# Two transformer layers on one core: a written-out TensorE order and a minimum of negated scores in the first attention

## Chip, core and metric

The kernel runs on one core of a Trainium2 chip. Its time is the device time in microseconds (us) of one execution; several executions are measured and the median is given. The core has five engines with a program order of their own: TensorE (PE, matrix products; PEld is its weight load), VectorE (DVE), ScalarE (ACT), GpSimd (POOL) and SyncE (SP), which here issues the DMAs.

## What is computed

`x` has 4 batch rows of 256 tokens and 256 features. Everything is float32. Two pre-norm layers follow one another, each an attention and a feed-forward network:

```python
x = x + _L0_attn_ref(_layernorm(x), ...)   # 16 query heads, 8 key heads, RMS norm, RoPE, window 128
x = x + _L0_ffn_ref(_layernorm(x), ...)    # silu gate, 2 of 4 kept
x = x + _L1_attn_ref(_layernorm(x), ...)   # 16 heads, causal
x = x + _L1_ffn_ref(_layernorm(x), ...)    # silu gate, Walsh-Hadamard transform
```

The first attention, on which the change works mostly:

```python
q = jnp.einsum('btd,ndh->btnh', x, q_kernel)
k, v = jnp.einsum('bsd,ckdh->cbskh', x, kv_kernel)
q, k = rms_norm(q, q_norm_scale), rms_norm(k, k_norm_scale)
q, k = apply_rope(q, positions), apply_rope(k, positions)
mask = (j <= i) & (i - j < 128)
logits = jnp.einsum('btkgh,bskh->bkgts', qg * ATTN_SCALE, k)
probs = jax.nn.softmax(jnp.where(mask, logits, finfo.min), axis=-1)
enc = jnp.einsum('bkgts,bskh->btkgh', probs, v)
return jnp.einsum('btnh,nhd->btd', enc, out_kernel)
```

## The kernel before

**Steps of the first attention.** The work is cut into 16 units, numbered n = 4 b + g: batch row b and group g of 4 query heads with their 2 key heads. `pipelined` runs a loop over steps. In each step every stage handles the unit that lies its lag behind the step:

- `project` (lag 0): for each of the two 128-token blocks, two products, 512 columns of queries (`wq`) and 512 columns of keys and values (`wkv`), each as two matmuls into a PSUM tile `pj` of the pool's tag "half" (four buffers, shared with `tr_q`). DVE then writes `pj` times the sine and the cosine table (`qs`, `qc`, L466), ACT squares it (`sq`, L471) and copies the values (`v`).
- `rotate` (lag 0): DVE adds `qc` and the swapped `qs` (L484) and sums the squares (`ss`, L485). POOL makes `r`, the power -1/2 of the twelve mean squares of a token (L498, L501, L504), and multiplies the keys by it (L507). The queries' factors stay in `r`. From n = 6 on POOL also splits the queries into 16-bit planes (`qpl`), which a DMA transposes (`qplT`).
- `turn` (lag 1): the queries are transposed by TensorE (`tr_q`, n < 6) or put together from the DMA's planes by DVE (`qT`); the keys by TensorE (`tr_k`, L533), copied to `kT` by ACT (L534).
- `score` (lag 2): for each half of two heads, `probabilities`. TensorE makes the scores `sc` (L218, L219), a custom DVE instruction adds the mask, writes the sums to `p` and keeps the row's maximum `mx` (L221); DVE makes the bias `nb` = -`mx` times `r` (L228), or times the constant scale in the second attention (L226); ACT takes exp with the scale `r` and the bias `nb` and sums the rows (L231); DVE takes the reciprocal `rs` (L236), POOL multiplies `p` by it (L239).
- `split` (lag 3) and `join` (lag 4): POOL splits `p` into planes (`pl`, L245), a DMA transposes them (`plT`), ACT copies them to `pT` (L265).
- `attend` (lag 4): TensorE multiplies with `v` (`av`, L409, L413), ACT copies to `zT`. `out` follows in `behind`: `po`, one token block of one half of a batch row (L300), and DVE adds it to `x`.

**The order of the work.** `order` says in which order a step's stages are written, `(0, 5, 4, 3, 1, 2, 6)` here: project, join, split, score, rotate, turn, attend. A scheduler of the framework then puts the instructions of each engine in an order of its own; `tc.issue_after` holds an instruction behind another, and `manual_schedule`, for the steps of `in_order`, keeps an engine to the written order. The first attention has no such steps before, the second has (for TensorE). Each engine executes its instructions in the order in which they were built.

**The norm.** `moments(b)` gives mean and reciprocal deviation of a batch row, `normed(b)` subtracts and scales on DVE (`xn`, L172), transposes on TensorE (`tr_n`, L183) and copies on ACT (`xnT`). The row b + 1 is normed in `project` of the row b, with g = 1 (moments) and g = 2:

```python
                if g == 2 and b + 1 < B:
                    with tc.issue_after(last_of["qc"].ins):
                        xnT[b + 1] = normed(b + 1, factors[b + 1])
```

The second attention uses `probabilities` too, with `rq` None. The functions that the diff touches, and what calls them:

Of the kernel before, what the change touches and what calls it, by code (L numbers as in the profile page):

```python
# [21 lines left out]
F32 = mybir.dt.float32  # L22
BF16 = mybir.dt.bfloat16
U16 = mybir.dt.uint16
AF = mybir.ActivationFunctionType
ALU = mybir.AluOpType
AX = mybir.AxisListType

P = 128
B, T, D = 4, 256, 256  # L30
NT = T // P
NC = D // P
HD = 128
# [3 lines left out]
WINDOW = 128  # L37
LN_EPS = 1e-5
RMS_EPS = 1e-6
SCALE0 = 0.08838834764831845  # L40
SCALE1 = 0.08838834764831845
NEG0 = -1e30
NEG1 = -1e10


C_ID, C_HAD, C_M0, C_M1, C_END = 0, 128, 256, 640, 1024
# [3 lines left out]
def two_layers(ctx, tc, consts, tables, x, wq, wkv, wo, w_gate, w_up, w_down,  # L50
               w_k, w_q, w_v, w_o, w1, w3, w2, out):
    nc = tc.nc
# [92 lines left out]
    last_of = {}  # L145
# [60 lines left out]
    def probabilities(qT, kT, heads, mask, rq=None):  # L206


        p = work.tile([P, 2, 3 * P], F32, tag="p", name="p", bufs=4)
        mx = small.tile([P, 2, 2], F32, tag="mx", name="mx")  # L210
        nb = small.tile([P, 2, 2], F32, tag="nb", name="nb")
        sm = small.tile([P, 2, 2], F32, tag="sm", name="sm")
        rs = small.tile([P, 2, 2], F32, tag="rs", name="rs")
        rows = ((0, slice(0, P)), (1, slice(P, 3 * P)))
        for j in range(2):
            q, k = qT[:, heads[j], :], kT[:, heads[j] if rq is None else heads[0] // 2, :]
            sc = bank([3 * P], "sc")
            nc.tensor.matmul(sc[:, 0:P], lhsT=q[:, 0:P], rhs=k[:, 0:P], start=True, stop=True)  # L218
            nc.tensor.matmul(sc[:, P : 3 * P], lhsT=q[:, P:T], rhs=k, start=True, stop=True)  # L219
            for i, cols in rows:  # L220
                last_of["mx"] = nc.vector.tensor_tensor_reduce(  # L221
                    out=p[:, j, cols], in0=sc[:, cols], in1=mask[:, cols], scale=1.0,
                    scalar=-3.0e38, op0=ALU.add, op1=ALU.max, accum_out=mx[:, j, i : i + 1],
                )
        if rq is None:
            nc.vector.tensor_scalar_mul(nb, mx, -SCALE1)  # L226
        else:
            nc.vector.scalar_tensor_tensor(nb, mx, -1.0, rq, ALU.mult, ALU.mult)  # L228
        for j in range(2):
            for i, cols in rows:  # L230
                last_of["exp"] = nc.scalar.activation(  # L231
                    p[:, j, cols], p[:, j, cols], AF.Exp, bias=nb[:, j, i : i + 1],
                    scale=SCALE1 if rq is None else rq[:, j, i : i + 1],
                    accum_out=sm[:, j, i : i + 1],
                )
        nc.vector.reciprocal(rs, sm)  # L236
        for j in range(2):
            for i, cols in rows:
                nc.gpsimd.tensor_scalar(  # L239
                    p[:, j, cols], p[:, j, cols], rs[:, j, i : i + 1], 1.0, ALU.mult, ALU.mult  # L240
                )
        return p
# [86 lines left out]
    def attention0():  # L329
        with tc.tile_pool(name="attn0", bufs=2, reuse_waits="tile", side="right") as own:  # L330
# [10 lines left out]
                            tab[:, t], src.unsqueeze(1).to_broadcast([P, 2, HD]), scl, ALU.mult  # L341
                        )

            def project(n, _):
                b, g = divmod(n, 4)
                held = project0(own, xnT[b], g, cos_s, sin_s, n == 0)
                if g == 1 and b + 1 < B:
                    factors[b + 1] = moments(b + 1)
                if g == 2 and b + 1 < B:
                    with tc.issue_after(last_of["qc"].ins):  # L350
                        xnT[b + 1] = normed(b + 1, factors[b + 1])
                return held if n < 14 else rotated(n, held)

            def rotated(n, held):
# [7 lines left out]
            def turn(n, held):  # L362
                rot, qT_planes, v, r = held
                return *turn0(own, rot, qT_planes, half if 6 <= n < 14 else bank), v, r

            def score(n, held):
                qT, kT, v, r = held
# [52 lines left out]
            def out(b, t, gs, kept=False):  # L420
# [12 lines left out]
                for b in range(B) for k in range(2) for t in range(NT)  # L433
            }
            behind = {step: fns for step, fns in behind.items() if step < 16}
            behind[17] = [lambda _: xn_f.append(normed(0))]
            behind[19] = [lambda _: xn_f.append(normed(1)), *(out(3, t, (2, 3)) for t in range(NT))]
            pipelined(
                (project, rotate, turn, score, split, join, attend), (0, 0, 1, 2, 3, 4, 4),
                behind, (0, 5, 4, 3, 1, 2, 6),  # L440
            )

    def project0(own, xnT, g, cos_s, sin_s, first):
# [9 lines left out]
        parts = [(t, *part) for t in range(NT) for part in (queries, rest)]  # L453
        if first:
            parts = [(t, *part) for part in (queries, rest) for t in range(NT)]
        for t, w, hs in parts:
            qc, qs, sq = rot[t]
            pj = half([4, HD], "pj")
            n = hs.stop - hs.start
            for c in range(NC):  # L460
                last_of[0] = nc.tensor.matmul(  # L461
                    pj, lhsT=xnT[:, c, t * P : (t + 1) * P], rhs=w[:, g, c, :],
                    start=(c == 0), stop=(c == NC - 1),
                )
            for rot_to, tab in ((qs, sin_s), (qc, cos_s)):
                last_of["qc"] = nc.vector.tensor_tensor(  # L466
                    rot_to[:, hs], pj[:, 0:n],
                    tab[:, t, hs.start // 4, :].unsqueeze(1).to_broadcast([P, n, HD]),
                    ALU.mult,
                )  # L470
            nc.scalar.activation(sq[:, hs], pj[:, 0:n], AF.Square)  # L471
            if n == 2:
                last_of["v", t] = nc.scalar.copy(v[:, t, :, :], pj[:, 2:4])
        return rot, v

    def rotate0(rot, by_dma, first):

# [10 lines left out]
        if by_dma:  # L488

            planes = page_of_planes([P, NT, 2, 4 * HD], "qpl")  # L490
            for t, qc in enumerate(rot):
# [3 lines left out]
            nc.sync.dma_start_transpose(qT_planes, planes.rearrange("p t w n -> p (t w n)"))  # L495

        ve = small.tile([P, NT, 6], F32, tag="ve", name="ve")
        nc.gpsimd.tensor_scalar(  # L498
            ve[:, :, 0:4], ss[:, :, 0:4], 1.0, HD * RMS_EPS, ALU.mult, ALU.add
        )  # L500
        nc.gpsimd.tensor_scalar(  # L501
            ve[:, :, 4:6], ss[:, :, 4:6], 1.0 / HD, RMS_EPS, ALU.mult, ALU.add
        )
        nc.gpsimd.tensor_tensor(r.rearrange("p t h -> p (t h)"), ve.rearrange("p t h -> p (t h)"),  # L504
                                mhalf, ALU.pow)
        for t, qc in enumerate(rot):
            last_of["k"] = nc.gpsimd.tensor_tensor(  # L507
                qc[:, 4:6, :], qc[:, 4:6, :],
                r[:, t, 4:6].unsqueeze(2).to_broadcast([P, 2, HD]), ALU.mult,
            )  # L510
        return rot, qT_planes, r

    def turn0(own, rot, qT_planes, bank_of_k):
# [3 lines left out]
        for t, qc in enumerate(rot):  # L517
# [13 lines left out]
            tk = bank_of_k([2, P], "tr_k")  # L531
            for j in range(2):
                nc.tensor.transpose(tk[:, j, :], qc[:, 4 + j, :], ident)  # L533
            nc.scalar.copy(kT[:, :, cols], tk)  # L534
        return qT, kT


# [554 lines left out]
def _constants():  # L1092
# [7 lines left out]
    while len(h) < P:  # L1100
        h = np.block([[h, h], [h, -h]])
    c[:, C_HAD:C_M0] = h / np.float32(32)
    for at, window, neg in ((C_M0, WINDOW, NEG0), (C_M1, T, NEG1)):
        for n, (qb, kb) in enumerate(((0, 0), (1, 0), (1, 1))):
            i = qb * P + np.arange(P)[:, None]
            j = kb * P + np.arange(P)[None, :]
            ok = (j <= i) & (i - j < window)
            c[:, at + n * P : at + (n + 1) * P] = np.where(ok, 0.0, neg)
    frac = np.arange(0, HD, 2, dtype=np.float32) / np.float32(HD)
    angle = np.arange(T, dtype=np.float32)[:, None] / np.power(np.float32(10000.0), frac)  # L1110
    angle = angle.astype(np.float32)
# [60 lines left out]
```

## Time and profile before

| | |
|---|---|
| median of 3 runs | 731.75 us (731.65 to 732.66) |
| the profiled execution | 733.21 us, of which the span is 731.4 us |
| granted TensorE clock | 1.00 |
| busy: PE, PEld | 718.4, 572.4 us |
| busy: DVE, ACT, POOL | 476.0, 414.0, 367.3 us |
| the first attention | from the start to about 262 us |

The span goes from the first to the last instruction. A group's row gives the line, the engine, the operation, what it writes and reads, the shape, the number of instructions, their busy time in us and the mean of one in ns, and behind the second bar how long the engine was idle before them and what ended that. Matmuls are pipelined and their ends are modelled, so a duration on PE includes time in which its successor already runs.

### The profile page before, as it was taken

The page shows a single profiled execution, that of the slowest core. Times are in us where ns is not written, and L with a number is a line of the kernel's source. Part 1 is how long each engine was busy: PE and PEld are TensorE (multiplying, and loading weights), DVE is VectorE, ACT ScalarE, POOL GpSimd, SP SyncE. Part 2 cuts the span into 40 slices and gives each one's busy share as a digit, 9 for nine tenths or more (in the row PEclk, how much of TensorE's full clock was granted, in tenths as well). Part 3 has the DMA queues.
Part 4 walks back from the last instruction along what each step waited for, and adds up shares of the span by engine and source line. Part 5 has one row for each costly group of instructions (what it writes and reads, how often), then busy time and mean ns, then how long its engine had stood idle before and what let it go on. Part 6 is the DMA issues. An engine that isn't in the chain of part 4 may idle for free. (4 is left out here: it accounts for less than half of the span.)

```text
span 731.4 us, 10484 instructions
## 1 busy us (share of the span) xinstructions
PE 718.4 (98%) x3336; PEld 572.4 (78%) x3336; DVE 476.0 (65%) x1425; ACT 414.0 (57%) x984; POOL 367.3 (50%) x521
## 2 busy tenths in 40 slices
PE   9999999999999999999999999999999999999998
PEld 5556566656666778888887899999998889888886
DVE  6999877788887536987844556665553554635443
ACT  2487887767767962222357655555555557654331
POOL 1678878897799741011105566473636663802000
PEclk9999999999999999999999999999999999999999
DMA  8732345425355447000003334252425422401000
GB/s 324 301 65 45 64 83 92 88 53 99 73 93 102 73 75 227 16 14 15 9 7 58 66 65 130 58 117 44 125 48 116 117 44 45 89 13 30 0 30 29
DMA packets 138342, 57.42 MB, mean 79 GB/s; under 512 B 131504, under 2 KB 133680, under 8 KB 137520
## 3 DMA queue, kind: packets, MB, share of 16 engines
q1 hardware_dynamic: 138288, 56.77, 34.6%
q8 instruction: 26, 0.43, 0.2%
q14 instruction: 28, 0.23, 0.1%
HBM read 22.94 MB, written 1.05 MB: 33 GB/s over the span
## 5 line engine op out<-in xcount | busy, mean ns | idle before, releaser
L239 POOL TENSOR_SCALAR p<-p,rs 128x128 f32<-128x128 f32 (+1 forms) x256 | 114.2, 465 | 137.1 <-DVE rs L236 137.1
L265 ACT COPY pT<-plT 128x1536 uint16<-128x1536 uint16 (+1 forms) x62 | 93.6, 1566 | 10.0 <-DMA plT<-pl 10.0
L245 POOL TENSOR_SCALAR pl<-p 128x1536 uint16<-128x1536 uint16 x64 | 94.4, 1476 | 4.6 <-POOL p L239 0.5
L221 DVE CUSTOM_DVE_ANT_0 p<-sc,cst 128x128 f32<-128x128 f32 (+1 forms) x256 | 78.7, 352 | 12.4 <-PE sc L219 10.0
L231 ACT ACTIVATE p<-p,nb,r 128x128 f32<-128x128 f32 (+1 forms) x128 | 68.2, 535 | 20.2 <-DVE nb L228 20.2
L461 PE MATMUL pj<-wq,xnT 128*128 128x512 f32 x128 | 61.0, 595 | 1.4 <-DVE qT L523 1.1
L231 ACT ACTIVATE p<-p,nb 128x128 f32<-128x128 f32 (+1 forms) x128 | 56.4, 442 | 9.7 <-DVE nb L226 9.7
L461 PE MATMUL pj<-wkv,xnT 128*128 128x512 f32 x128 | 60.1, 592 | 0.0
L300 PE MATMUL po<-wo,zT 128*128 128x256 f32 x256 | 57.9, 379 | 0.0
L471 ACT ACTIVATE sq<-pj 128x512 f32<-128x512 f32 (+1 forms) x64 | 30.9, 490 | 42.8 <-DVE qc L466 42.4
L157 POOL TENSOR_SCALAR ve<-mv 128x2 f32<-128x2 f32 (+1 forms) x17 | 4.3, 253 | 99.6 <-DVE mv L153 99.0
L725 ACT COPY qk<-qk_x 128x512 f32<-128x512 f32 x16 | 9.4, 586 | 78.6 <-PE qk_x L945 42.0
L300 PEld LDWEIGHTS po<-wo,zT 128*128 128x128 f32 x256 | 48.3, 190 | 7.0 <-ACT kT L534 0.6
L461 PEld LDWEIGHTS pj<-wkv,xnT 128*128 128x128 f32 x128 | 24.3, 190 | 30.2 <-issue 28.5
L466 DVE TENSOR_TENSOR qs<-pj,sin_s 128x512 f32<-128x512 f32 (+1 forms) x64 | 35.3, 551 | 13.5 <-PE pj L461 12.9
L461 PEld LDWEIGHTS pj<-wq,xnT 128*128 128x128 f32 x128 | 23.5, 190 | 24.5 <-issue 20.1
L273 PE MATMUL av<-pT,v 128*128 128x256 f32 x128 | 38.4, 381 | 0.2 <-ACT zT L817 0.2
L245 POOL TENSOR_SCALAR qpl<-qc 128x1024 uint16<-128x1024 uint16 x20 | 28.8, 1453 | 18.9 <-PE av L413 8.2
L219 PE MATMUL sc<-kT,qT 128*128 128x256 f32 x128 | 38.3, 381 | 0.0
L219 PE MATMUL sc<-qk 128*128 128x256 f32 x128 | 38.2, 380 | 0.0
L854 DVE TENSOR_TENSOR x<-po,x 128x128 f32<-128x128 f32 x56 | 16.0, 285 | 33.1 <-PE po L849 33.1
L504 POOL TENSOR_TENSOR r<-ve,mhalf 128x12 f32<-128x12 f32 x16 | 36.6, 2290 | 0.8
(187 smaller groups left out, 1797.6 us busy)
## 6 DMA issues: line engine op xcount, KB each, us to landing
w<-in_w_dram SPq DMA_DIRECT2D x3, 1024.0 KB, 5.5
wq<-in_wq_dram SPq DMA_DIRECT2D x4, 512.0 KB, 7.6
wkv<-in_wkv_dram SPq DMA_DIRECT2D x4, 512.0 KB, 8.2
wo<-in_wo_dram SPq DMA_DIRECT2D x4, 512.0 KB, 10.2
w_qk<-in_w_q_dram SPq DMA_DIRECT2D x4, 512.0 KB, 4.3
w_qk<-in_w_k_dram SPq DMA_DIRECT2D x4, 512.0 KB, 5.2
w_v<-in_w_v_dram SPq DMA_DIRECT2D x4, 512.0 KB, 6.4
w_o<-in_w_o_dram SPq DMA_DIRECT2D x4, 512.0 KB, 6.3
```

The costliest lines, as they stand in the source:

```text
L219: nc.tensor.matmul(sc[:, P : 3 * P], lhsT=q[:, P:T], rhs=k, start=True, stop=True)
L221: last_of["mx"] = nc.vector.tensor_tensor_reduce(out=p[:, j, cols], in0=sc[:, cols], in1=mask[:, cols], scale=1.0, scalar=-3.0e38, op0=ALU ...
L231: last_of["exp"] = nc.scalar.activation(p[:, j, cols], p[:, j, cols], AF.Exp, bias=nb[:, j, i : i + 1], scale=SCALE1 if rq is None else rq ...
L239: nc.gpsimd.tensor_scalar(p[:, j, cols], p[:, j, cols], rs[:, j, i : i + 1], 1.0, ALU.mult, ALU.mult)
L245: last_of["planes"] = nc.gpsimd.tensor_scalar(o, i, 1.0, 1.0, ALU.mult, ALU.mult)
L265: copy(words.rearrange("p (n w) -> p w n", w=2), halves[:, :, js].rearrange("p w j n -> p w (j n)"),)
L273: nc.tensor.matmul(av, lhsT=v0, rhs=pT[:, 0:T], start=True, stop=False, skip_group_check=True)
L300: nc.tensor.matmul(po, lhsT=zTs[hd // 4][:, hd % 4, t * P : (t + 1) * P], rhs=w[:, hd, :], start=(hd == 0), stop=(hd == n - 1),)
L461: last_of[0] = nc.tensor.matmul(pj, lhsT=xnT[:, c, t * P : (t + 1) * P], rhs=w[:, g, c, :], start=(c == 0), stop=(c == NC - 1),)
L466: last_of["qc"] = nc.vector.tensor_tensor(rot_to[:, hs], pj[:, 0:n], tab[:, t, hs.start // 4, :].unsqueeze(1).to_broadcast([P, n, HD]), AL ...
L471: nc.scalar.activation(sq[:, hs], pj[:, 0:n], AF.Square)
L504: nc.gpsimd.tensor_tensor(r.rearrange("p t h -> p (t h)"), ve.rearrange("p t h -> p (t h)"), mhalf, ALU.pow)
```

## The change

In words:

1. `project` is cut into `begin` (token block 0) and the rest (block 1). The written order of a step becomes begin, join, split, score, project (the rest), rotate, turn, attend, so that the scores of unit n - 2 stand between the two blocks' projections of unit n. For unit 0 all four parts stay in `begin`.
2. TensorE keeps this written order in the steps 0 to 16 (`in_order` is `(0, 17)`).
3. `moments(b + 1)` is issued after the last `qc`, and `normed(b + 1)` moves from `project` to the end of the steps 2, 6 and 10 (`next_norm` in `behind`).
4. In `rotate0` the power is split for the units below 6: first the keys' mean and power, then the products with the keys, then the queries' mean and power. From unit 6 on it stays one power of 12 elements.
5. The keys' copy `kT` gets the scale -1, so that the scores are negated, and the mask of the first attention has +1e30 instead of -1e30. The DVE instruction multiplies by `r` (or by the negated constant scale in the second attention) and keeps the minimum `mn`, which is the bias of exp at once; exp has the constant scale -1. `nb` and its instruction go, in both attentions.

The diff:

```diff
--- before.py
+++ after.py
@@ -39,7 +39,7 @@
 RMS_EPS = 1e-6
 SCALE0 = 0.08838834764831845
 SCALE1 = 0.08838834764831845
-NEG0 = -1e30
+FAR0 = 1e30
 NEG1 = -1e10
 
 
@@ -207,8 +207,7 @@
 
 
         p = work.tile([P, 2, 3 * P], F32, tag="p", name="p", bufs=4)
-        mx = small.tile([P, 2, 2], F32, tag="mx", name="mx")
-        nb = small.tile([P, 2, 2], F32, tag="nb", name="nb")
+        mn = small.tile([P, 2, 2], F32, tag="mn", name="mn")
         sm = small.tile([P, 2, 2], F32, tag="sm", name="sm")
         rs = small.tile([P, 2, 2], F32, tag="rs", name="rs")
         rows = ((0, slice(0, P)), (1, slice(P, 3 * P)))
@@ -219,19 +218,15 @@
             nc.tensor.matmul(sc[:, P : 3 * P], lhsT=q[:, P:T], rhs=k, start=True, stop=True)
             for i, cols in rows:
                 last_of["mx"] = nc.vector.tensor_tensor_reduce(
-                    out=p[:, j, cols], in0=sc[:, cols], in1=mask[:, cols], scale=1.0,
-                    scalar=-3.0e38, op0=ALU.add, op1=ALU.max, accum_out=mx[:, j, i : i + 1],
+                    out=p[:, j, cols], in0=sc[:, cols], in1=mask[:, cols],
+                    scale=-SCALE1 if rq is None else rq[:, j, i : i + 1],
+                    scalar=3.0e38, op0=ALU.add, op1=ALU.min, accum_out=mn[:, j, i : i + 1],
                 )
-        if rq is None:
-            nc.vector.tensor_scalar_mul(nb, mx, -SCALE1)
-        else:
-            nc.vector.scalar_tensor_tensor(nb, mx, -1.0, rq, ALU.mult, ALU.mult)
         for j in range(2):
             for i, cols in rows:
                 last_of["exp"] = nc.scalar.activation(
-                    p[:, j, cols], p[:, j, cols], AF.Exp, bias=nb[:, j, i : i + 1],
-                    scale=SCALE1 if rq is None else rq[:, j, i : i + 1],
-                    accum_out=sm[:, j, i : i + 1],
+                    p[:, j, cols], p[:, j, cols], AF.Exp, bias=mn[:, j, i : i + 1],
+                    scale=-1.0, accum_out=sm[:, j, i : i + 1],
                 )
         nc.vector.reciprocal(rs, sm)
         for j in range(2):
@@ -341,14 +336,16 @@
                             tab[:, t], src.unsqueeze(1).to_broadcast([P, 2, HD]), scl, ALU.mult
                         )
 
-            def project(n, _):
+            def begin(n, _):
                 b, g = divmod(n, 4)
-                held = project0(own, xnT[b], g, cos_s, sin_s, n == 0)
+                return project0(own, xnT[b], g, cos_s, sin_s, n == 0)
+
+            def project(n, begun):
+                b, g = divmod(n, 4)
+                held = begun()
                 if g == 1 and b + 1 < B:
-                    factors[b + 1] = moments(b + 1)
-                if g == 2 and b + 1 < B:
                     with tc.issue_after(last_of["qc"].ins):
-                        xnT[b + 1] = normed(b + 1, factors[b + 1])
+                        factors[b + 1] = moments(b + 1)
                 return held if n < 14 else rotated(n, held)
 
             def rotated(n, held):
@@ -362,6 +359,12 @@
             def turn(n, held):
                 rot, qT_planes, v, r = held
                 return *turn0(own, rot, qT_planes, half if 6 <= n < 14 else bank), v, r
+
+            def next_norm(b):
+                def emit(_):
+                    with tc.issue_after(last_of["qc"].ins):
+                        xnT[b] = normed(b, factors[b])
+                return emit
 
             def score(n, held):
                 qT, kT, v, r = held
@@ -433,11 +436,13 @@
                 for b in range(B) for k in range(2) for t in range(NT)
             }
             behind = {step: fns for step, fns in behind.items() if step < 16}
+            for b in range(1, B):
+                behind.setdefault(4 * b - 2, []).append(next_norm(b))
             behind[17] = [lambda _: xn_f.append(normed(0))]
             behind[19] = [lambda _: xn_f.append(normed(1)), *(out(3, t, (2, 3)) for t in range(NT))]
             pipelined(
-                (project, rotate, turn, score, split, join, attend), (0, 0, 1, 2, 3, 4, 4),
-                behind, (0, 5, 4, 3, 1, 2, 6),
+                (begin, project, rotate, turn, score, split, join, attend),
+                (0, 0, 0, 1, 2, 3, 4, 4), behind, (0, 6, 5, 4, 1, 2, 3, 7), (0, 17),
             )
 
     def project0(own, xnT, g, cos_s, sin_s, first):
@@ -453,7 +458,11 @@
         parts = [(t, *part) for t in range(NT) for part in (queries, rest)]
         if first:
             parts = [(t, *part) for part in (queries, rest) for t in range(NT)]
-        for t, w, hs in parts:
+        def some(parts):
+            for part in parts:
+                one(*part)
+
+        def one(t, w, hs):
             qc, qs, sq = rot[t]
             pj = half([4, HD], "pj")
             n = hs.stop - hs.start
@@ -471,7 +480,12 @@
             nc.scalar.activation(sq[:, hs], pj[:, 0:n], AF.Square)
             if n == 2:
                 last_of["v", t] = nc.scalar.copy(v[:, t, :, :], pj[:, 2:4])
-        return rot, v
+        def rest_of_it():
+            some(() if first else parts[2:])
+            return rot, v
+
+        some(parts if first else parts[:2])
+        return rest_of_it
 
     def rotate0(rot, by_dma, first):
 
@@ -495,19 +509,27 @@
             nc.sync.dma_start_transpose(qT_planes, planes.rearrange("p t w n -> p (t w n)"))
 
         ve = small.tile([P, NT, 6], F32, tag="ve", name="ve")
-        nc.gpsimd.tensor_scalar(
-            ve[:, :, 0:4], ss[:, :, 0:4], 1.0, HD * RMS_EPS, ALU.mult, ALU.add
-        )
-        nc.gpsimd.tensor_scalar(
-            ve[:, :, 4:6], ss[:, :, 4:6], 1.0 / HD, RMS_EPS, ALU.mult, ALU.add
-        )
-        nc.gpsimd.tensor_tensor(r.rearrange("p t h -> p (t h)"), ve.rearrange("p t h -> p (t h)"),
-                                mhalf, ALU.pow)
+        halves = mhalf.rearrange("p (t h) -> p t h", t=NT)
+        keys, queries, both = slice(4, 6), slice(0, 4), slice(0, 6)
+
+        def power(hs):
+            nc.gpsimd.tensor_tensor(r[:, :, hs], ve[:, :, hs], halves[:, :, hs], ALU.pow)
+
+        def mean(hs, scale, eps):
+            nc.gpsimd.tensor_scalar(ve[:, :, hs], ss[:, :, hs], scale, eps, ALU.mult, ALU.add)
+
+        mean(keys, 1.0 / HD, RMS_EPS)
+        if by_dma:
+            mean(queries, 1.0, HD * RMS_EPS)
+        power(both if by_dma else keys)
         for t, qc in enumerate(rot):
-            last_of["k"] = nc.gpsimd.tensor_tensor(
-                qc[:, 4:6, :], qc[:, 4:6, :],
-                r[:, t, 4:6].unsqueeze(2).to_broadcast([P, 2, HD]), ALU.mult,
+            nc.gpsimd.tensor_tensor(
+                qc[:, keys, :], qc[:, keys, :],
+                r[:, t, keys].unsqueeze(2).to_broadcast([P, 2, HD]), ALU.mult,
             )
+        if not by_dma:
+            mean(queries, 1.0, HD * RMS_EPS)
+            power(queries)
         return rot, qT_planes, r
 
     def turn0(own, rot, qT_planes, bank_of_k):
@@ -531,7 +553,7 @@
             tk = bank_of_k([2, P], "tr_k")
             for j in range(2):
                 nc.tensor.transpose(tk[:, j, :], qc[:, 4 + j, :], ident)
-            nc.scalar.copy(kT[:, :, cols], tk)
+            nc.scalar.activation(kT[:, :, cols], tk, AF.Copy, scale=-1.0)
         return qT, kT
 
 
@@ -1100,12 +1122,12 @@
     while len(h) < P:
         h = np.block([[h, h], [h, -h]])
     c[:, C_HAD:C_M0] = h / np.float32(32)
-    for at, window, neg in ((C_M0, WINDOW, NEG0), (C_M1, T, NEG1)):
+    for at, window, far in ((C_M0, WINDOW, FAR0), (C_M1, T, NEG1)):
         for n, (qb, kb) in enumerate(((0, 0), (1, 0), (1, 1))):
             i = qb * P + np.arange(P)[:, None]
             j = kb * P + np.arange(P)[None, :]
             ok = (j <= i) & (i - j < window)
-            c[:, at + n * P : at + (n + 1) * P] = np.where(ok, 0.0, neg)
+            c[:, at + n * P : at + (n + 1) * P] = np.where(ok, 0.0, far)
     frac = np.arange(0, HD, 2, dtype=np.float32) / np.float32(HD)
     angle = np.arange(T, dtype=np.float32)[:, None] / np.power(np.float32(10000.0), frac)
     angle = angle.astype(np.float32)
```

## The prediction

> **What bounds the kernel now.** I read the page first, then the table by stretches of time, TensorE's waits, the timelines of single engines, and last the groups with shapes kept apart. The page:
>
> ```profile
> PE 718.4 (98%) x3336; PEld 572.4 (78%) x3336; DVE 476.0 (65%) x1425; ACT 414.0 (57%) x984; POOL 367.3 (50%) x521
> DVE  6999877788887536987844556665553554635443
> ```
>
> TensorE is busy for 98% of the span, so a change to the other engines can only win where TensorE waits. The rows by stretch (columns PE, PEld, DVE, ACT, POOL, clock, DMA share, GB/s) show that DVE is as full as TensorE early on:
>
> ```profile
> 20.00:40.00 20.00, 18.60 (x74) 10.70 (x73) 19.11 (x48) 10.39 (x32) 12.48 (x17) 1.00 0.60 240
> 40.00:60.00 20.00, 19.09 (x83) 12.20 (x82) 19.64 (x61) 15.34 (x41) 15.49 (x22) 1.00 0.32 60
> 80.00:100.00 20.00, 19.90 (x79) 12.43 (x78) 14.77 (x40) 14.68 (x33) 18.68 (x27) 1.00 0.42 78
> 240.00:262.00 22.00, 20.85 (x98) 16.20 (x97) 13.34 (x52) 20.90 (x45) 16.00 (x25) 1.00 0.51 82
> ```
>
> TensorE's waits (us in total, times, longest), and its timeline near the end of the first attention:
>
> ```profile
> PE av L409 <- DVE mx L221: 2.2, 3, 0.8
> PE tr_k L533 <- POOL qc L507: 1.6, 2, 1.2
> PE pj L461 <- DVE qT L523: 1.1, 2, 0.9
> ```
>
> ```profile
> 243.64 0.60 PE L533 MATMUL tr_k<-cst,qc 128*128 128x128 f32 x4
> 245.04 1.10 PE L409 MATMUL av<-pT,v 128*128 128x512 f32 x2 [0.81 <-DVE mx L221]
> 247.70 1.89 PE L300 MATMUL po<-wo,zT 128*128 128x256 f32 x8
> 249.43 0.38 PE L218 MATMUL sc<-kT,qT 128*128 128x128 f32 x2
> ```
>
> Durations overlap, so I measure from start to start: the eight po instructions take 249.43 - 247.70 = 1.73, 0.216 each. In the same way 128 columns take 0.109 and 512 take 0.429. Four tr_k should last 0.44 but av starts 1.40 later: a gap of 0.97. Done for every instruction, the gaps are 3.1 us before 20 us (mostly the idle matmuls), 4.5 after 262, and between them 9.2: tr_k 1.36 at 22.4; pj 0.47 at 38.4 and 1.17 at 50.3; av 1.09 at 72.3; small ones 0.53 at 82 to 84; 1.18 at 148 to 150; av 0.79 at 218; av 1.85 from 245 to 255; the rest, 0.8, crumbs. These 9.2 us are all that the new order can win.
>
> **Prices.** Groups of the first 262 us, shapes apart (busy and mean ns, then idle before):
>
> ```profile
> L265 ACT COPY pT<-plT 128x1536 uint16<-128x1536 uint16 x29 | 54.3, 1925 | 0.0
> L504 POOL TENSOR_TENSOR r<-ve,mhalf 128x12 f32<-128x12 f32 x16 | 36.6, 2290 | 0.8
> L484 DVE TENSOR_TENSOR qc<-qc,qs 128x768 f32<-128x768 f32 x32 | 32.6, 1022 | 0.1
> L231 ACT ACTIVATE p<-p,nb,r 128x128 f32<-128x128 f32 x64 | 31.0, 484 | 20.2 <-DVE nb L228 20.2
> L485 DVE TENSOR_REDUCE ss<-sq 128x6 f32<-128x768 f32 x32 | 30.0, 940 | 4.2 <-ACT sq L471 4.1
> L172 DVE TENSOR_SCALAR xn<-x,mv,rstd 128x256 f32<-128x256 f32 x12 | 5.7, 503 | 3.2 <-PE tr_n L183 2.0 <-POOL rstd L158 1.0
> ```
>
> In units of TensorE time a projection is 6.87 (3.43 per token block), four heads' scores 2.62, a turn 1.31 (0.44 once the queries go by DMA), av 2.57, one po block 1.72, tr_n 0.44. A step of TensorE work is 10.8 before the first av (steps 2 and 3), 13.4 in steps 4 and 5, 14.2 from step 6.
>
> **Part by part.** S2 means the start of step 2, and so on; the order on each engine is the built one.
>
> *Removed: the 9.2 us.* With the scores 3.43 us earlier in a step, the last mx is ready well before av, so the av waits go; the other gaps belong to the old order and I take them all away, then add the new ones.
>
> *Arithmetic.* 64 nb instructions leave DVE (32 of 293 ns in the first attention). The scale of exp becomes a constant: 484 ns with the r operand against 390 in the second attention's rows, 94 x 128 = 12 us of ACT. Both lie beside TensorE's work, so they are worth only what they shorten a wait; cover gone, nb is 0.07 to 0.29 per half. In the second attention the gaps are under 1 us each: gain 0 to 0.6, I take 0.3. In the first, DVE's score instruction now takes its scale from r per partition; no row shows that. Nearest is xn (two such operands, 0.41 alone) against 0.42 for a 256-wide two-tensor product with none: 0. Upper bound: the 0.094 that ACT pays, x 8 a step; lower bound 0, as the same elements are read. The row on the same engine decides: 0.
> The Trainium skill ("ScalarE: Activation LUTs", What ACT_TABLE_LOAD costs) gives about 93 ns for each per-partition pointer operand, on ScalarE; ACT's rows agree. Carried to DVE it would add 1.5 us in steps 2 and 3, an estimate; DVE's own row speaks against that.
>
> *tr_k(0), at 22 us.* Before, POOL ran two means (0.20 each) and one power (2.29) ahead of the key products. The power is split: from 2290 ns for 12 elements and 712 for 2 I work out 0.158 per element, so 1.03 for 4 and 1.66 for 8. As built, both powers still stand ahead of the products, so the chain is 0.4 longer; a score wait of 0.2 comes with it. But turn 0 comes later on TensorE, behind sc and block 1. Stall 0.3 to 1.8, I take 1.2 for both.
>
> *Step 2, tr_n.* Before, xn went at 31.06, ahead of the reduces:
>
> ```profile
> 31.06 0.73 DVE L172 TENSOR_SCALAR xn<-x,mv,rstd 128x256 f32<-128x256 f32 x2
> 31.70 1.81 DVE L485 TENSOR_REDUCE ss<-sq 128x6 f32<-128x768 f32 x2
> ```
>
> Now xn stands last in the step on DVE, and tr_n last in the step on TensorE, in written order. After block 1's last matmul DVE has two 256-wide evictions (0.33 each), two adds and two reduces (0.87 alone, 1.02 and 0.94 in the mean), two qT copies (0.60) and xn (0.41): 5.75 alone, 6.2 at the means. TensorE has turn 1 in that time, 1.31. Stall 4.4 to 4.9, with DVE late 5.3: I take 4.8. Queued behind tr_n is the whole of pj(3). At steps 6 and 10 DVE has 5 us per step free (14.77 of 20) and TensorE has av and po before tr_n: 0 to 0.5.
>
> *Step 4, pj.* Its first product takes the PSUM half that pj(3) block 1 left, free when ACT has squared it. As built that square stands behind eight exps and both copies of pT (L265). Exps start at S3 + 4.9 (block 0 3.43, half the scores 1.31, first mask 0.2), last 3.6, the copies 2 x 1.79 from start to start, the square 0.5, its release 0.2: S3 + 12.8. TensorE gets there at 3.43 + 2.62 + 3.43 + 1.31 = S3 + 10.8. Stall 2.0 (1.6 to 2.8). From step 5 only one copy stands there and a step is 13.4 to 14.2: 0.8 to 3 us spare, 0 to 0.8 in all, I take 0.4.
>
> *End, step 16.* tr_k(15) needs POOL's key products of step 15. POOL in order from S15 + 6.85 (rs): p 2.05, pl 1.45, qpl 1.45, p 1.6, pl 1.45, qpl 1.4, means 0.55, power 2.3, products 0.6 and 0.6: S15 + 19.7 and 20.3. TensorE, with no projection left in step 16: pj 6.87, sc 2.62, tr_k(14) 0.44, av 2.57, po 1.72, sc(14) 2.62 = S15 + 16.8. Stall 3.0 with the second product half covered, and 0.4 for a score's qT: 3.4 (2.5 to 4.5). Queued behind it are av, sc(15) and the last out; before, the products ended at 238.2 and tr_k came at 243.64.
>
> *Sum.* 1.2 + 4.8 + 2.0 + 0.4 + 3.4 = 11.8, and 0.6 for crumbs (the old order had as much): 12.4; 12.4 - 9.2 - 0.3 = +2.9. The profiled execution took 733.21 (span 731.4, 1.8 around it), so it would become 736.1; the median is 731.75, 1.46 lower, so **734.6**.
>
> The Trainium skill ("Perfetto Trace Analysis", Identifying the Most-Contended Engine) would judge the kernel by LDWEIGHTS time, 78% here, not by matmul time: that would leave up to 159 us to win. The start-to-start rows leave 17. By the page a better order may be worth much; by the rows at most the 9.2.
>
> **Rivals.**
> *A, faster: the lumps do not add.* While TensorE stands 4.8 us in step 2, ACT and POOL catch up, so step 4's wait nearly goes (0.5), and at the end POOL runs at its fastest rows (qpl 1.05 at 230.8, p 1.63), which takes 1.2 off, and rs comes 0.6 earlier: 1.6. Then 1.0 + 4.4 + 0.5 + 0 + 1.6 + 0.3 = 7.8 - 9.2 - 0.6 = -2.0: 729.8. It begins to win once the three waits make less than 7.3 (10.2 in my sum). For it: POOL is at 16.00 of 22 there. Against: step 2's queue is DVE work that no one else can take.
> *B, slower by more: the pointer scale costs DVE 0.094 each.* Steps 2 and 3 are DVE's, 38.75 of 40 busy: 16 x 0.094 = 1.5 on top, and the ends of the other terms 1 more: 737.
> *C, it does not do what it says.* "Keys first" is not what POOL gets, see above; if the key chain were the short one (0.2 + 1.03 + 0.6 instead of 0.4 + 2.69 + 0.6), tr_k(0) would not wait: 733.4.
>
> **Numbers.** My forecast 0.60, A 0.17, B 0.13, C 0.10. Upper ends of all terms give 1.8 + 5.3 + 2.8 + 0.8 + 4.5 + 0.6 = 15.8; less 9.2 is +6.6, 738.3; the lower ends 0.3 + 4.4 + 1.6 + 0 + 2.5 - 0.6 = 8.2, 730.7, and a little of A below that: 730.0 to 738.3. About 0.2%, 1.46 us, can be told from no change. Faster takes most of A: 0.14; same the rest of A, a sixth of the forecast and some of C: 0.20; slower 0.66.
>
> **What would show it.** In the profile after: tr_n at about 38.7 us waiting for DVE xn some 4.8; the first pj of step 4 waiting for ACT sq 2; the last tr_k waiting for POOL qc 3; no av waiting for the score instruction; the score instruction as long as L221's 286 and 417 ns. I am wrong if xn is done with turn 1, if the score instruction is over 350 and 480, or if TensorE's gaps between 20 and 262 us sum to under 9.

## The result, and the profile after

The changed kernel takes 739.43 us in the median of 4 runs (739.15 to 740.61), against 732.16 (731.65 to 732.66) of the kernel before. The ratio is 1.0099, with a 95% interval of 1.0087 to 1.0112: slower by 1.0%. The forecast was slower, 734.6, with a range up to 738.3; the sign was right, and the size was less than half.

The two profiled executions took 733.21 and 739.15, 5.9 apart. The rest of the 7.3 us between the medians is that the profiled execution before was one of the longer ones, and that of after one of the shorter. What follows explains the 5.9.

The page of the changed kernel: busy times, and two rows of its forty slices.

```profile
PE 718.9 (97%) x3336; PEld 575.5 (78%) x3336; DVE 478.0 (65%) x1361; ACT 397.9 (54%) x984; POOL 386.4 (52%) x527
PE   9879999999999899999999999999999999999998
PEclk9989999999999999999999999999999999999999
```

TensorE's work is the same, but it has holes in the second and third slice and in the fourteenth, and the granted clock is lower in the third. ACT lost 16.1 us of busy time and POOL gained 19.1; what that is worth has to be read from TensorE's waits. These waits (us in total, times, longest) name the holes:

```profile
PE tr_n L183 <- DVE xn L172: 5.5, 1, 5.5
PE tr_k L555 <- POOL qc L526: 3.4, 2, 2.8
PE pj L470 <- ACT sq L480: 1.8, 1, 1.8
```

These are the three waits of the forecast, in the places it gave. No `av` waits for the score instruction any more, and from 56 to 239 us TensorE has no gap over 0.15 us. Start to start, as in the prediction, the gaps between 20 and 262 us sum to 15.4 us (9.2 before). TensorE's timeline at the first of the three, and at the last:

```profile
33.48 0.38 PE L555 MATMUL tr_k<-cst,qc 128*128 128x128 f32 x2
39.34 1.11 PE L183 MATMUL tr_n<-cst,xn 128*128 128x128 f32 x4 [5.47 <-DVE xn L172]
40.24 3.38 PE L470 MATMUL pj<-wq,xnT 128*128 128x512 f32 x4
43.46 1.88 PE L470 MATMUL pj<-wkv,xnT 128*128 128x512 f32 x4
```

```profile
248.27 1.26 PE L555 MATMUL tr_k<-cst,qc 128*128 128x128 f32 x4 [2.80 <-POOL qc L526]
249.32 1.06 PE L295 MATMUL po<-wo,zT 128*128 128x256 f32 x2
```

Here is what the forecast did not have. The four `pj` instructions after the first wait take 43.46 - 40.24 = 3.22 us, 0.81 each, where four take 1.72 at the usual 0.429; after the last wait `po` takes 0.43 each instead of 0.216. The four `tr_n` are slow too, 0.21 each instead of 0.109. The products behind the first wait run at half pace for 3.9 us, those behind the last for 3.2. The table by stretches (PE, PEld, DVE, ACT, POOL, clock, DMA share, GB/s) shows the granted clock in them:

```profile
40.00:44.00 4.00, 4.00 (x9) 1.89 (x8) 0.34 (x1) 0.58 (x1) 3.24 (x4) 0.59 0.55 102
36.45:43.20 6.75, 3.87 (x8) 2.22 (x9) 3.15 (x6) 0.58 (x1) 6.42 (x8) 0.50 0.50 92
248.20:252.00 3.80, 3.73 (x10) 2.40 (x11) 1.98 (x2) 0.77 (x2) 3.71 (x7) 0.57 0.31 59
```

TensorE is "busy" for the whole of 40 to 44 and yet works at about half its pace. The trace's clock record has 0.50 from 36.43 to 43.25 and from 248.05 to 251.47, and 1.00 elsewhere between 20 and 262: the clock falls during each wait, and comes back 3.9 and 3.2 us after the products do.

DVE in step 2, from the end of block 1's evictions, and POOL beside it:

```profile
33.27 1.79 DVE L498 TENSOR_TENSOR qc<-qc,qs 128x768 f32<-128x768 f32 x1
34.98 0.94 DVE L499 TENSOR_REDUCE ss<-sq 128x6 f32<-128x768 f32 x1
35.84 1.05 DVE L498 TENSOR_TENSOR qc<-qc,qs 128x768 f32<-128x768 f32 x1
36.83 0.94 DVE L499 TENSOR_REDUCE ss<-sq 128x6 f32<-128x768 f32 x1
38.88 0.72 DVE L172 TENSOR_SCALAR xn<-x,mv,rstd 128x256 f32<-128x256 f32 x2
```

```profile
32.78 1.47 POOL L240 TENSOR_SCALAR pl<-p 128x1536 uint16<-128x1536 uint16 x1
34.23 3.02 POOL L234 TENSOR_SCALAR p<-p,rs 128x128 f32<-128x128 f32 x4
```

The queue is the one that the prediction listed, in its order, but the first add takes 1.79 us and not 0.95. DVE's next instruction starts 0.73 after POOL's `pl` ends, as if the add had hardly moved before; and POOL's four divisions of `p`, 1.63 at 31.06, where DVE works on `pj`, take 3.02.

The score instruction, last, with shapes apart, in the first attention:

```profile
L220 DVE CUSTOM_DVE_ANT_0 p<-sc,cst,r 128x256 f32<-128x256 f32 x64 | 30.3, 473 | 0.0
L220 DVE CUSTOM_DVE_ANT_0 p<-sc,cst,r 128x128 f32<-128x128 f32 x64 | 22.1, 345 | 1.8 <-PE sc L218 1.5 <-POOL pl L240 0.3
```

473 and 345 ns, against 417 and 286 with the constant scale: the scale that is read per partition costs DVE 56 to 59 ns an instruction. The second attention does the same with a constant scale and stays at 418 and 287, so it is not the minimum that costs.

### The profile page after: what moved, and what is told of

Its sections match the earlier page's. It is cut to its first block, busy times and chain, and to the rows that moved or that the text cites. A ratio compares the mean times of both kernels' runs of the same rounds, so it can differ in the third digit from the quotient of the medians.

```text
span 737.4 us, 10376 instructions
## 1 busy us (share of the span) xinstructions
PE 718.9 (97%) x3336; PEld 575.5 (78%) x3336; DVE 478.0 (65%) x1361; ACT 397.9 (54%) x984; POOL 386.4 (52%) x527
## 4 chain that ended last, share of the span: by engine, by line
PE 51%; POOL 24%; issue 15%; DVE 5%; ACT 3%; DMA 2%; SPq 0%; POOLq 0%; DVEq 0%; ACTq 0%
POOL p L234 9%; PE pgu L587 7%; PE pj L470 7%; POOL pl L240 5%; PE po L295 5%; PE po_f L634 4%; PE gu_x L1044 4%; PE po L280 3%; PE po_f L658 3%; PE sc L218 2%; PE av L412 2%; PE gu_y L1044 2%; POOL r L516 2%; PE qk_x L967 2%; POOL qpl L240 2%
## 5 line engine op out<-in xcount | busy, mean ns | idle before, releaser
L234 POOL TENSOR_SCALAR p<-p,rs 128x128 f32<-128x128 f32 (+1 forms) x256 | 138.8, 559 | 139.9 <-DVE rs L231 139.1
L227 ACT ACTIVATE p<-p,mn 128x128 f32<-128x128 f32 (+1 forms) x256 | 112.6, 446 | 3.2 <-DVE mn L220 3.2
L260 ACT COPY pT<-plT 128x1536 uint16<-128x1536 uint16 (+1 forms) x62 | 95.2, 1569 | 10.9 <-DMA plT<-pl 10.0
L227 ACT ACTIVATION_READ_ACCUMULATOR p<-p,mn 128x1 f32 x256 | 49.2, 192 | 0.0
L220 DVE CUSTOM_DVE_ANT_0 p<-sc,cst,r 128x128 f32<-128x128 f32 (+1 forms) x128 | 45.1, 409 | 1.8 <-PE sc L218 1.5
L220 DVE CUSTOM_DVE_ANT_0 p<-sc,cst 128x128 f32<-128x128 f32 (+1 forms) x128 | 38.3, 352 | 10.1 <-PE sc L218 8.2
L516 POOL TENSOR_TENSOR r<-ve,mhalf 128x12 f32<-128x12 f32 (+2 forms) x22 | 38.5, 1758 | 1.3
L498 DVE TENSOR_TENSOR qc<-qc,qs 128x768 f32<-128x768 f32 x32 | 38.6, 1206 | 0.0
```

The costliest lines, as they stand in the source:

```text
L220: last_of["mx"] = nc.vector.tensor_tensor_reduce(out=p[:, j, cols], in0=sc[:, cols], in1=mask[:, cols], scale=-SCALE1 if rq is None else r ...
L227: last_of["exp"] = nc.scalar.activation(p[:, j, cols], p[:, j, cols], AF.Exp, bias=mn[:, j, i : i + 1], scale=-1.0, accum_out=sm[:, j, i : ...
L234: nc.gpsimd.tensor_scalar(p[:, j, cols], p[:, j, cols], rs[:, j, i : i + 1], 1.0, ALU.mult, ALU.mult)
L260: copy(words.rearrange("p (n w) -> p w n", w=2), halves[:, :, js].rearrange("p w j n -> p w (j n)"),)
L498: nc.vector.tensor_tensor(parts[0], parts[0], parts[1][:, :, ::-1, :], ALU.add)
L516: nc.gpsimd.tensor_tensor(r[:, :, hs], ve[:, :, hs], halves[:, :, hs], ALU.pow)
```

## The experiments

The theory after the result: the written order brings three waits, two of them long enough to lower TensorE's clock, and DVE's queue ahead of the first is lengthened by POOL. The rivals: the slow products come from transfers beside them; the waits are DVE's lack of time and would only move; the arithmetic causes them. The kernels of one comparison shared the runs of the kernel before (732.8 to 732.9 in the median). That is 0.6 to 0.7 us above the 732.16 beside which 739.43 was measured, so a difference to 739.43 is uncertain by as much. Each ratio is to the kernel before. The diffs are shortened, and comments in them are added.

**TensorE kept awake.** Products of zeroes stand in the two long waits:

```diff
+            for i in range(idle_before if t == 0 else 0):      # 11 in step 2, ahead of tr_n
+                nc.tensor.matmul(
+                    tr[:, i % 2, :], lhsT=zeroes[:, 0:P], rhs=zeroes, start=True, stop=True
+                )
...
+            for i in range(12 if last and t == 0 else 0):      # ahead of tr_k(15)
+                nc.tensor.matmul(
+                    tk[:, i % 2, :], lhsT=zeroes[:, 0:P], rhs=zeroes[:, P:], start=True, stop=True
+                )
```

> The changed kernel with TensorE kept at work in its two long waits: 11 products of zeroes (128x256) ahead of tr_n in step 2, written into tr_n's own PSUM tile, and 12 (128x128) ahead of the last tr_k; the transposes write over them, so nothing else changes. Theory (the granted clock falls because TensorE stands idle, 0.59 and 0.57 of full speed in the 4 us after each wait): the two waits stay as long as they are (tr_n still starts 5.8 us after turn 1 is over), but the products after them run at full pace: 1.5 us less at each, 3.0 in all, 736.4 us, granted clock 1.00. Rival (they are slow because of the weights' DMAs that run beside them): no change, 739.4 us, clock 0.99.

Measured: 736.32 us (736.07 to 736.34), ratio 1.0044 (1.0032 to 1.0057), mean clock 1.00. Two rows of its table, the first stretch again and the last wait with its fill:

```profile
40.00:44.00 4.00, 4.00 (x13) 2.06 (x13) 1.72 (x4) 1.18 (x2) 3.24 (x4) 1.00 0.53 98
243.00:248.20 5.20, 4.93 (x36) 3.98 (x35) 1.71 (x11) 5.18 (x17) 4.98 (x9) 1.00 0.96 178
```

`tr_n` starts at 39.34 as before, so the wait is as long; the transfers are as many (0.53 of the DMA engines against 0.55), and the clock is 1.00. So TensorE's idleness lowers its clock, not the transfers. It was worth 3.1 us between the medians and 2.8 between the profiled executions, about as much as the whole net loss that was forecast; in the trace a score at 250 now starts 1.04 us late, mostly for DVE's `rs`, and takes a part back. Useless work made the kernel faster.

**xn early.** The scaling goes back ahead of the adds, the transposes stay:

```diff
+                if g == 2 and b + 1 < B:      # in project, before rotate
+                    with tc.issue_after(last_of["qc"].ins):
+                        factors[b + 1] = scaled(b + 1, factors[b + 1])   # xn alone
...
-                    with tc.issue_after(last_of["qc"].ins):
-                        xnT[b] = normed(b, factors[b])
+                    xnT[b] = transposed(factors[b])                      # tr_n and xnT
```

> The changed kernel with the scaling xn put ahead of the adds and reduces on DVE again in the steps 2, 6 and 10, while its transposes tr_n stay at the end of the step on TensorE. Theory (tr_n waits only because xn stands last on DVE): tr_n starts with turn 1's end, and 5.8 us of wait and 1.5 us of slow clock after it go. DVE's 6 us of queued work are still there, and pj(3)'s block 1 or the scores will wait for it: 1 to 3 us come back; 734 us (732 to 735.5). Rival (DVE as a whole is the limit in steps 2 and 3): the wait only moves to sc(1), which needs the qT copies behind the same queue, or to pj(3)'s PSUM half; 737.5 to 739.4 us.

Measured: 733.72 us (732.07 to 735.08), ratio 1.0010 (1.0001 to 1.0019). `tr_n`'s gap is 0.76 us and no slow clock follows; `sc(1)` now waits 0.75 for `qT`, and step 4's `pj` 1.13 instead of 1.94. The wait was a matter of place in DVE's queue, and little of it came back. The wait at the end is still there (2.98 us); in the profiled execution, the longest of the eleven, the clock was 0.50 for 6.8 us behind it, while the shortest had a mean clock of 0.999.

**Unit 0's copies late.**

```diff
-                        slice(0, 2), last_of["exp"],
+                        slice(0, 2), last_of["v3"] if n == 0 else last_of["exp"],
```

`v3` is ACT's last instruction on `pj(3)`.

> The changed kernel with the two copies of pT of unit 0 held behind ACT's work on pj(3) block 1. Theory: the first pj of step 4 no longer waits 1.9 us for ACT's square; the copies still end before av(0): 737.5 us. Rival (the square then waits for DVE's qc, or sc(2) for kT, so that the wait has another name): 738.5 to 739.5 us.

Measured: 737.02 us (736.24 to 739.15), ratio 1.0059 (1.0045 to 1.0072). The `pj` of step 4 has no gap, and no new wait follows it before the end. But the 2.4 us are not this wait alone. At the end the wait of 2.97 us is as long as before, and here the products behind it run at full pace, with a granted clock of 1.00:

```profile
246.91 1.01 PE L557 MATMUL tr_k<-cst,qc 128*128 128x128 f32 x4 [2.81 <-POOL qc L528]
247.76 0.60 PE L295 MATMUL po<-wo,zT 128*128 128x256 f32 x2
```

So a wait of this length brings the slow clock in one execution and not in another. The clock records show what decides: in all thirteen traces of this case the changes of the clock lie whole multiples of 3.41 us apart. In the changed kernel 2.7 us of the wait lie in one such stretch, from 244.64 to 248.05; here a border at 245.80 cuts it into 1.9 and 1.1. Before every fall TensorE had stood idle for 2.4 us or more of one stretch, and at the full clock 2.04 or less brought no fall.

**The end.** In step 16 attend is written ahead of turn:

```diff
-                for k in order:
+                for k in order if step < 16 else last_order or order:
...
+                (0, 6, 5, 4, 1, 2, 7, 3),     # last_order
```

> The changed kernel with attend ahead of turn in TensorE's written order of step 16 alone, so that av(12), 2.57 us, stands between sc(14) and tr_k(15). Theory (nothing stands behind POOL's key products but this wait): the wait of 3.0 us falls to 0 to 0.6, and with it the slow clock after it (1.5 us): 735 us (734.7 to 736). Rival (what is left behind tr_k is so little that scores of unit 15, pT and av(15) then wait, since POOL's chain for unit 15 ends no earlier): 737 to 739 us.

Measured: 736.50 us (735.59 to 737.93), ratio 1.0054 (1.0041 to 1.0068), 1.5 us above the expectation; the profiled execution, the shortest of the five, took 735.59. Its TensorE timeline:

```profile
247.67 1.01 PE L556 MATMUL tr_k<-cst,qc 128*128 128x128 f32 x4 [0.23 <-POOL qc L527]
248.51 1.89 PE L295 MATMUL po<-wo,zT 128*128 128x256 f32 x8
```

The wait fell from 2.97 to 0.39 plus 0.29 between the two key blocks, and eight `po` take 1.73 again: the place is mended, with the slow clock. In this trace the gaps between 240 and 262 us went from 4.65 to 1.21. What is missing lies elsewhere: the second attention's two `qk_x` waits have 3.3 us here and 2.8 in the changed kernel; why they differ was not tried. The two executions with a mean clock of 0.998 took 735.59 and 736.34, the three with 0.995 took 736.50 to 737.93, so the rest goes, presumably, with how long the clock stayed low behind `tr_n`.

**The arithmetic alone**, in the old order (part 5 of the change put into the kernel before):

> The kernel before with part 5 alone: negated keys, minimum, bias without nb, constant scale of exp; stages and orders as before. Theory (the order costs all, the arithmetic little): DVE's score instruction takes 57 ns more than before (345 and 473 against 286 and 417 ns in the changed kernel), 8 a step make 0.46, nb gave about 0.2 to 0.4 back; within 1.5 us of before, 731 to 733.5 us. Rival B of the prediction (DVE bounds steps 2 and 3, and the pointer scale is what lengthens them): 734 us or more.

Measured: 732.56 us (732.01 to 734.87), ratio 1.0002 (0.9993 to 1.0011): no difference between the medians. In the trace `av` gaps of about 1 us at 72 and 245 are gone, and waits of `tr_k` for POOL are longer, 1.98 instead of 1.36 at 22 and 2.13 instead of 0.58 at 149:

```profile
149.32 1.18 PE L528 MATMUL tr_k<-cst,qc 128*128 128x128 f32 x4 [1.96 <-POOL qc L502]
```

Behind the last of these the clock is 0.50 from 150.02 to 153.43. Seven of the eleven executions have a clock of 1.00 and took 732.01 to 732.77; four, this one among them, have 0.998 and took 733.74 to 734.87. Whether the dearer score instruction and the missing `nb` by themselves cancel was not tried.

**The order alone** (the changed kernel with `mx`, `nb` and the scale `r` in exp):

> The changed kernel with the old arithmetic (mx, nb, scale r in exp): the written order, the split power and the moved norm alone. Theory: all three waits are there, of 5.5, 2 and 3 us with a slow clock after the first and the last; 738.5 to 740.5 us. Rival (the arithmetic makes them long): below 736 us.

Measured: 737.51 us (736.73 to 738.00), ratio 1.0063 (1.0050 to 1.0076). The expectation had three waits; there are two. `tr_n` waits 6.77 us with a slow clock after it; at the end `tr_k` waits 1.67 and the products after it keep their pace; step 4 has hardly any (0.16). ACT's timeline shows why:

```profile
53.62 0.57 ACT L485 ACTIVATE sq<-pj 128x512 f32<-128x512 f32 x1
54.34 1.92 ACT L265 COPY pT<-plT 128x1536 uint16<-128x1536 uint16 x1
```

The square stands ahead of the copies of `pT` here. In the changed kernel the scheduler had put both copies first, presumably because the new arithmetic's chain is shorter. So the arithmetic costs nothing by itself in the old order, but 1.9 us between the medians in the new one: ACT's built order is another, the last wait is 2.97 instead of 1.67 us, and the slow clock follows it; `tr_n`'s wait, 5.63 instead of 6.77, goes the other way.

**POOL beside DVE.** Two kernels with one execution each. First the changed kernel without the division of unit 0:

> The changed kernel without POOL's division of the probabilities by their row sums for unit 0 (this part of the computation is left out). Theory (DVE's add L498 took 1.71 us instead of 0.87 in step 2 because POOL read and wrote p beside it): in step 2 the first add takes 0.87 to 0.95 again and tr_n starts 0.8 to 1.0 us earlier; the wait is 4.6 to 4.8 us instead of 5.6. Rival (the add is slow for another reason, ACT or TensorE beside it): add 1.7 us, wait 5.6 us.

Measured: the first add still takes 1.59, `tr_n`'s gap is 5.32 and the time 739.69 us: the expectation failed, the division is not what holds the add. But without it POOL's `pl` ran 0.2 earlier, to 34.06, and DVE's next instruction started 0.73 after that again. So the split itself was moved:

```diff
+        with tc.issue_after(first.ins) if first else nullcontext():   # first: unit 2's last power, for unit 0
             copy_gpsimd(s, words.rearrange("p (n w) -> p w n", w=2))
```

> The changed kernel with POOL's split pl of unit 0 (1.47 us each half) held behind the powers of unit 2, so that POOL has no pl at work while DVE does the adds of step 2. Theory (DVE's two-input add stands still while POOL's pl runs: in the changed kernel pl ends at 34.25 and the add at 34.98, without the division pl ends at 34.06 and the add at 34.79, 0.73 later both times): the first add takes 0.87 to 1.1 instead of 1.79, xn and tr_n come 0.7 to 0.9 earlier, the wait is 4.7 to 4.9 instead of 5.6, the 4.8 of the forecast. Rival (the division p, which runs beside the adds too, slows them as much): add over 1.4, wait over 5.3. The later split may make the copies of pT of unit 0 late and step 4's wait longer; that is not what is asked.

Measured, DVE and POOL of that kernel:

```profile
32.97 1.16 DVE L499 TENSOR_TENSOR qc<-qc,qs 128x768 f32<-128x768 f32 x1
34.92 0.94 DVE L499 TENSOR_TENSOR qc<-qc,qs 128x768 f32<-128x768 f32 x1
```

```profile
30.76 4.06 POOL L234 TENSOR_SCALAR p<-p,rs 128x128 f32<-128x128 f32 x8 [1.45 <-DVE rs L231]
40.04 1.47 POOL L240 TENSOR_SCALAR pl<-p 128x1536 uint16<-128x1536 uint16 x1
```

The add takes 1.16, the second 0.94, and `tr_n`'s gap is 4.89, against the forecast's 4.8. The time is 738.88 us in one run. So it is POOL's long copy that holds DVE's add until it has ended; beside the short divisions the add loses 0.2. The Trainium skill ("SBUF — State Buffer", SBUF: two separate sides) says that a GpSimd instruction and a VectorE instruction with two SBUF inputs lock a common port pair, the first to start for the whole of its length. The end of the add, which follows that of the copy in both traces, agrees. But POOL's power in the kernel before, 2.27 us from 34.14 on, did not hold the add that DVE began beside it at 35.75 (0.95). By the page's rule it would have; in these traces not every POOL instruction does this.

**The three edits at once** (xn early, unit 0's copies late, attend first in step 16):

> The changed kernel with the three edits at once: xn early in the steps 2, 6 and 10, unit 0's copies of pT behind ACT's work on pj(3), attend ahead of turn in step 16. Theory (the new order's waits are these three and their slow clock; the old order's 9.2 us stay away): 739.4 - 7.3 - 1.9 - 4.5 = 725.7 if nothing comes back, 727 to 730 with what DVE's queue gives back in steps 2 to 4. Rival (the waits are taken over by the next in the queue): 732 us or more, no better than before.

Measured: 731.40 us (730.96 to 732.21), ratio 0.9981 (0.9973 to 0.9990): 8 us better than the changed kernel, but only 0.2% better than the kernel before. The expectation was too hopeful. Two of its waits:

```profile
PE sc L241 <- DVE qT L574: 1.4, 2, 1.1
PE sc L242 <- DVE qT L578: 1.2, 1, 1.2
```

The next in DVE's queue take over a part: at 39 and 51.5 scores wait for `qT`, which stands behind the adds and reduces. The 1.2 us of L242 are another place, the end at 245.5, and are as long in the next kernel.

**And turn ahead of rotate**, so that `qT` is copied before them:

```diff
-                (0, 0, 0, 1, 2, 3, 4, 4), behind, (0, 6, 5, 4, 1, 2, 3, 7), (0, 17),
+                (0, 0, 0, 1, 2, 3, 4, 4), behind, (0, 6, 5, 4, 1, 3, 2, 7), (0, 17),
```

> The kernel with the three edits (xn early, unit 0's copies late, attend first in step 16) and turn ahead of rotate in the written order, so that DVE copies qT before it does the adds and reduces. Theory (sc waited for qT behind them, 0.75 us at 39 and 1.55 at 51.5): both waits go, 2.3 us less, 729 us (728.5 to 730). Rival (the adds then come 1.2 later, POOL's powers and key products too, and tr_k or av waits): 731 us or more.

Measured: 730.36 us (729.72 to 731.12), ratio 0.9968 (0.9956 to 0.9980), the lowest median of all. The waits for `qT` at 39 and 51.5 are gone; 0.83 of them came back as a wait of `pj` for ACT's square, and 0.28 at `tr_n`, whose `xn` (1.52 us for two) runs beside POOL's `pl`.

**With the late split too:**

> As the kernel before it in this list, with POOL's split of unit 0 behind the powers of unit 2 as well. Theory (xn, 1.51 us for two where it took 0.73, is held by pl just as the add was): tr_n's last 0.76 us of wait goes, 728 to 729 us. Rival (the later split makes the copies of pT late, and av(0) or ACT's squares wait): 730 us or more.

Measured: 730.74 us (730.60 to 731.34), ratio 0.9973 (0.9963 to 0.9983). `xn` takes 0.89 and `tr_n`'s gap falls from 1.04 to 0.41, but `tr_k` waits 2.0 at 57.7: POOL comes to the key products at 57.07, 55.36 in the kernel ahead of it. It is another wait than the rival's two, but as the rival said nothing was gained; the intervals of the two kernels overlap.

## Why the prediction was wrong in size

Its steps against the gaps of the profile after (start to start, us):

| step of the sum | forecast | measured |
|---|---|---|
| `tr_k(0)` and the score behind it | 1.2 | 0.73 + 0.18 |
| step 2, `tr_n` | 4.8 | 5.63 + 0.05 |
| slow clock after it | not seen | 1.92 |
| step 4, `pj` | 2.0 | 1.94 |
| steps 5 to 14 | 0.4 | 0 |
| end, `tr_k(15)` | 3.4 | 2.97 + 0.20 |
| slow clock after it | not seen | 1.48 |
| crumbs | 0.6 | 0.30 |
| sum, 20 to 262 us | 12.4 | 15.4 |
| less the old gaps | -9.2 | -9.2 |
| second attention | -0.3 | -0.2 |

- The mechanism was right in each of its parts: the old order's 9.2 us all went, and three waits came, at DVE's `xn`, ACT's square and POOL's key products. The lengths read out of the built order and the durations before were within 0.5 us for two of them.
- The step that failed is the sum itself: it counted a wait as only its own length, and the products behind it at full pace. Two of the three are followed by 3.2 to 3.9 us at half pace, which cost 3.4 us in this trace; keeping TensorE awake brought 3.1 us back (739.43 to 736.32), with a clock of 1.00. The trace before had no hint: its longest gap between products is 1.36 us, and its clock 1.00 throughout. The Trainium skill ("TensorE: Matmul & The Clock Gate", What's actually happening) gives half rate after an idle window of about 3.4 us, and about 3.4 us of work to return; the wait of 4.8 us in the forecast called for it. The trace agrees on the half rate (0.50) and on a first wait long enough for it. But the last wait, 2.97 us, is shorter than the page's window and was enough too; a wait of 2.97 us was not enough in the kernel with unit 0's copies late, and 2.13 us were enough in that with the arithmetic alone. Every one of the six waits of 4.9 us and more had the slow clock behind it. For waits of 2 to 3 us the length alone does not tell.
- The term for `tr_n` was mis-sized by 0.9. The prediction took the add at its mean; beside `pl` it took 1.79. Before, POOL raised its powers at that time, and the adds took 0.95. With the split out of the way the wait was 4.89.
- A reading was wrong without harm: 14.77 of 20 us leaves DVE 5.2 us free in 20 us, which is 3.7 in a step of 14.2 and not 5. Steps 6 and 10 had no wait all the same.
- Rival B was half right on the instruction (56 to 59 ns and not 0; 94 was its bound), and wrong on the time: the arithmetic alone left the median where it was. The forecast's price of 0 for the scale read per partition was wrong by these 56 to 59 ns; what share of a wait is theirs was not measured.
- Rival A did not come: the wait of step 2 did not shorten those of step 4 (1.94) and the end (2.97).
- Rival C was right that both powers run before the key products, but turn 0 then waited 0.73, less than before.

## What to carry to other kernels

An engine's written order should be laid against the queues of the engines that feed it: an operand that stands last in DVE's queue and first in TensorE's costs the whole queue. A wait of about 5 us on TensorE is priced at its length and 1.5 to 2.5 us more, as the traces here had it (an estimate for other kernels); a wait of 2 to 3 us may cost as much in one execution and nothing more than its length in another. A fill of useless products is a quick way to see which part is which. After every change of a dependency the built order of the other engines is read again, since the scheduler may answer the change with another order.

## What was not expected of the hardware

- The granted clock changes in steps of 3.41 us: it fell to 0.50 where TensorE was idle for 2.4 us or more of such a stretch, and stayed there for 3.41 or 6.83 us. So a wait of 2.96 to 2.98 us lowered the clock in four traces and not in a fifth, and one of 2.13 us lowered it.
- POOL's copy of 128x1536 16-bit elements holds a DVE add of two SBUF operands until it ends (1.79 for 0.95 us), and `xn` is longer beside it too (1.51 for 0.73 for two). POOL's short divisions lose to DVE instead: they took 3.02 for 1.63 us, and the adds beside them lost only 0.1 to 0.2.
- DVE's custom score instruction takes 56 to 59 ns more with a scale read per partition, while ACT's exp takes about 90 less with a constant one (395 for 484 at 128 columns, 498 for 587 at 256).
